# Window attention with a routed feed-forward: score products visit the column halves in turn

## The chip, the cores and the metric

The kernel runs on one core of one Trainium2 chip. The metric is device time in microseconds (us) of one execution. TensorE (PE) does matrix products; it loads a stationary operand (PEld) and then streams a moving operand against it. VectorE is DVE, ScalarE is ACT, GpSimd is POOL, and SyncE (SP) starts most of the DMAs.

## The reference

The input x has 2 images of 128 channels and 256 x 256 pixels, in f32. One layer is computed:

```
x = x + conv(layer_norm_over_channels(x))
t = x as tokens of 128 channels
t = t + ffn(layer_norm(t))
```

`conv` is attention in windows with four heads of 32 channels. Queries come from windows of 8 x 8 pixels, keys and values from overlapping windows of 12 x 12, and a relative position term and a fixed mask are added to the scores:

```
attn = einsum('bnd,bmd->bnm', q * SCALE, k)
attn = attn + rel_pos_emb(q) + FIXED_MASK      # 0 or -inf
attn = softmax(attn);  out = einsum('bnm,bmd->bnd', attn, v);  W_out on top
```

The mask is -inf wherever the row or the column distance of query and key has one of the two parities. A pixel therefore attends only to pixels of fixed row and column parity, and the image falls into four independent planes of half the height and half the width. `ffn` is a routing over 8 experts: softmax, the best two, and the sum of these two experts' products, weighted.

## The kernel before

The image is cut into 64 strips of 8 rows (32 per image). Each strip has 4 planes (the parities), so the main loop runs over 256 steps `n`, one plane each. A plane of a strip has 4 rows of 128 columns, 512 pixels, in 16 windows of 8 columns (`NP = 16`, `HP = 8` of them in each half). A window sees 6 rows of 10 columns of keys, 60 keys, held in a slot of 64 (`SLOT`).

The main loop writes the order of the instructions by hand (a manual schedule over PE, DVE, ACT, Pool and SP), and mixes pieces of several steps: the scores of plane `n`, its attention and output projection, the projections of plane `n + 1`, and the norms, routing and expert products of neighbouring strips. Nothing is reordered by a scheduler. From step 6 on, an alignment at the head of each step puts TensorE's instructions at a fixed place in blocks of 256.

On TensorE a step is, in this order: key-mask products of the scores (L474), score products (L491), value projections (L350), the projections for relative terms, keys and queries (L409, L423, L445), four expert products (L714), softmax sums (L512), attention products (L522), norm statistics (L580), three expert products, the output projection (L550), and a last expert product.

The change touches `scores`. Scores lie with the keys on the partitions: the tile `att` has 128 partitions, 64 for the left half of the windows and 64 for the right half, and four PSUM banks, one for each head. The first 256 columns of a bank hold the queries of 8 windows, 32 each.

- L474 adds the relative terms and the mask. There are two turns `w`, and in each turn 8 products, over `half` and then over head `h`. A product has 32 rows of the array (the head's channels), 64 columns (the slot) and a moving operand of 128 columns.
- L491 adds query times key. For each of the 8 window places `t` there are 8 products, over `half` and then over `h`. A product has the head's 32 rows, 64 columns (the window's keys `kk`) and a moving operand of 32 columns (the window's queries `qs`). Each of the eight pairs (`h`, `half`) is a part of its own in the array: 4 groups of 32 rows by 2 halves of 64 columns. There are 64 such products per step. All products are f32, and each f32 product is two instructions for loading and two for multiplying, in the order load, multiply, load, multiply.
- L499, on ACT, takes the exp of all scores and writes `pT`.

`attend` is not changed. Its L512 and L522 use parts of the other shape: 64 rows (the keys of a half) by 32 columns (a head's channels). L522 has 64 products per step, for each `t` over `half` and then over `h`, each with a moving operand of 32 columns.

Of the kernel before, what the change touches and what calls it, by code (L numbers as in the profile page):

```python
# [18 lines left out]
HEADS, DH = 4, 32  # L19
# [26 lines left out]
SLOT = 64  # L46
# [5 lines left out]
def kernel(  # L52
# [21 lines left out]
    HP = NP // 2  # L74
# [111 lines left out]
    for h in range(HEADS):  # L186
        hp = slice(h * DH, (h + 1) * DH)
# [67 lines left out]
    def place(i, k):  # L255

        return (PR * strips[i][1] + k) % KR
# [204 lines left out]
    def scores(n, state):  # L462


        qs, kk, au = state["qs"], state["kk"], state["au"]
        turn = place(n // 4, 0) // 2
        att = ps_att.tile([P, 4, 512], F32, tag="att", name=f"att{n}")
        sc = att[:, :, 0:HQ]
        for w in range(2):
            for half in range(2):  # L470
                rows = slice(half * SLOT, (half + 1) * SLOT)
                for h in range(HEADS):
                    hp = slice(h * DH, (h + 1) * DH)
                    nc.tensor.matmul(  # L474
                        sc[rows, h].rearrange("p (t w z) -> p t w z", w=2, z=16)[:, :, w],
                        lhsT=keys[hp, turn, w],
                        rhs=au[hp, half * NP + w : (half + 1) * NP : 2].rearrange(
                            "p t a s -> p t (a s)"
                        ),
                        start=(w == 0),  # L480
                        stop=False,
                    )
        for t in range(HP):
            if t == HP // 2:
                yield
            for half in range(2):
                rows = slice(half * SLOT, (half + 1) * SLOT)
                m0 = 2 * (half * HP + t)
                for h in range(HEADS):
                    hp = slice(h * DH, (h + 1) * DH)  # L490
                    nc.tensor.matmul(  # L491
                        sc[rows, h, 32 * t : 32 * t + 32],
                        lhsT=kk[hp, half * HP + t, :],
                        rhs=qs[hp, m0 : m0 + 2].rearrange("p m a s -> p (m a s)"),
                        start=False,
                        stop=(t == HP - 1),
                    )
        pT = work.tile([P, HEADS, HQ], F32, tag="pT", name=f"pT{n}", bufs=1)
        nc.scalar.activation(pT, att[:, :, 0:HQ], AF.Exp)  # L499
        state.update(att=att, pT=pT)  # L500
        yield
# [306 lines left out]
    with tc.manual_schedule(engines={ET.PE, ET.DVE, ET.Activation, ET.Pool, ET.SP}):  # L808
        for n in range(n_planes + 7):
            i, pl = divmod(n, 4)  # L810
            score, attn, outp, ahead, norm, rout = none, none, none, none, none, none
            if n < n_planes:
                score = scores(n, states[n])
                attn = attend(n, states[n])
                outp = out_project(n, states[n])
# [146 lines left out]
```

## Time and profile before

| what | value |
|---|---|
| time, median of 3 runs | 4331.74 us (4326.62 to 4331.98) |
| the profiled execution | 4321.7 us, span 4319.9 us |
| mean granted TensorE clock | 0.992 |
| PE busy | 4217.3 us, 98% of the span |
| PE weight loads busy | 2466.8 us, 57% |
| DVE busy | 3852.5 us, 89% |
| ACT busy | 1452.8 us, 34% |
| POOL busy | 1086.0 us, 25% |
| expert products L714, PE | 1915.4 us in 4096 instructions |
| score products L491, PE | 400.6 us in 32768 instructions |
| attention products L522, PE | 345.1 us in 32768 instructions |
| key-mask products L474, PE | 179.8 us in 8192 instructions |

Busy time is the time in which at least one instruction of a kind is under way; the mean duration of one instruction can be far longer than its share of the busy time, since TensorE works on many small products at once. The span runs from the first to the last instruction of the program. "Releaser" is what ended an engine's wait; "issue" stands for time without a wait that the profile shows.

### The profile page before, as it was taken

The numbers are of one execution on the slowest core, as the hardware profiler recorded it, in microseconds if no ns is written. First come the engines' busy times: TensorE is split into PE (matmuls) and PEld (weight loads), VectorE is DVE, ScalarE is ACT, GpSimd is POOL, SyncE is SP. The second block draws the span as 40 slices with busy tenths as digits, with TensorE's granted clock in tenths as the row PEclk, the third lists the DMA queues.
The fourth block names the chain that finished last, engine by engine and source line by source line (L and its number), as shares of the span: only waits on it lengthen the run. The fifth ranks groups of instructions, "written<-read, shape, count | busy, mean of one in ns | idle before, by whom it ended". The sixth has DMA issues, their size and how long they took to land. (4 is left out here: it accounts for less than half of the span.)

```text
span 4319.9 us, 224653 instructions
## 1 busy us (share of the span) xinstructions
PE 4217.3 (98%) x94273; PEld 2466.8 (57%) x94273; DVE 3852.5 (89%) x11850; ACT 1452.8 (34%) x3774; POOL 1086.0 (25%) x1126
## 2 busy tenths in 40 slices
PE   7899999999999999999999999999999999999987
PEld 4455555555555555555555555555555555555553
DVE  4799999999999999999999999999999999999977
ACT  3333333333333333333333333333333333333321
POOL 1222222222222222222222222222222222222211
PEclk9999999999999999999999999999999999999999
DMA  3678777787777777778787777777778787877765
GB/s 109 209 236 247 240 247 242 241 246 242 245 242 244 247 240 248 243 239 247 241 248 240 246 243 243 245 242 246 241 243 244 240 250 238 247 247 241 243 193 191
DMA packets 824580, 1022.19 MB, mean 237 GB/s; under 512 B 137634, under 2 KB 409634, under 8 KB 823594
## 3 DMA queue, kind: packets, MB, share of 16 engines
q1 hardware_dynamic: 822864, 1007.52, 75.4%
q8 instruction: 769, 12.60, 1.3%
q14 instruction: 217, 1.78, 0.1%
q10 hardware_dynamic: 730, 0.29, 0.0%
HBM read 863.78 MB, written 143.75 MB: 233 GB/s over the span
## 5 line engine op out<-in xcount | busy, mean ns | idle before, releaser
L714 PE MATMUL acc<-xe,ew 128*128 128x512 f32 x4096 | 1915.4, 600 | 18.6 <-DVE gb L688 16.5
L714 PEld LDWEIGHTS acc<-xe,ew 128*128 128x128 f32 x4096 | 758.1, 190 | 936.6 <-issue 886.5
L705 DVE TENSOR_TENSOR xe<-xs,gb 128x512 f32<-128x512 f32 x1536 | 950.6, 686 | 11.1 <-DMA gb<-gd 1.1
L709 POOL COPY last<-xe 128x1 f32<-128x1 f32 x256 | 47.1, 184 | 3113.7 <-DVE gb L688 3107.2
L705 POOL TENSOR_TENSOR xe<-xs,gb 128x512 f32<-128x512 f32 x512 | 650.6, 1272 | 1.5 <-PE att L522 0.7
L491 PE MATMUL att<-qs,kcol 32*64 32x32 f32 x32768 | 400.6, 226 | 11.1 <-issue 10.8
L434 ACT COPY kcol<-pk 128x560 f32<-128x560 f32 (+2 forms) x344 | 318.8, 927 | 275.3 <-PE pk L423 272.5
L491 PEld LDWEIGHTS att<-qs,kcol 32*64 32x64 f32 x32768 | 396.7, 131 | 13.9 <-issue 13.6
L276 POOL TENSOR_TENSOR xn<-xt,rb 128x512 f32<-128x512 f32 x249 | 373.7, 1501 | 91.1 <-DMA rb<-gd 74.6
L522 PEld LDWEIGHTS att<-pT,vwin 64*32 64x32 f32 x32768 | 348.6, 105 | 40.8 <-issue 3.2
L522 PE MATMUL att<-pT,vwin 64*32 64x32 f32 x32768 | 345.1, 200 | 2.4 <-issue 2.2
L499 ACT ACTIVATE pT<-att 128x1024 f32<-128x1024 f32 x256 | 261.9, 1023 | 180.3 <-PE att L491 180.1
L350 PE MATMUL pv<-wt,xn 128*128 128x128 f32 x2048 | 301.1, 291 | 0.9 <-issue 0.9
L574 ACT ACTIVATE sq<-xt 128x512 f32<-128x512 f32 x505 | 291.8, 629 | 0.0
L397 DVE STREAM_TRANSPOSE au<-auT 128x512 f32<-128x512 f32 x256 | 272.1, 1063 | 9.0
L550 PE MATMUL po<-o,wt 128*128 128x512 f32 x512 | 264.9, 599 | 9.5 <-DVE o L542 5.9
L409 PE MATMUL pu<-xn,wrel 128*128 128x512 f32 x512 | 266.2, 602 | 1.2 <-issue 1.2
L445 PE MATMUL pq<-xn,wt 128*128 128x512 f32 x512 | 261.9, 592 | 0.9 <-issue 0.8
L423 PE MATMUL pk<-xn,wt 128*128 128x512 f32 (+2 forms) x528 | 261.4, 578 | 0.0
L350 PEld LDWEIGHTS pv<-wt,xn 128*128 128x128 f32 x2048 | 251.7, 193 | 11.8 <-issue 1.3
L474 PEld LDWEIGHTS att<-au,keys 32*64 32x64 f32 x8192 | 118.9, 132 | 234.0 <-PE po L550 181.1
L413 DVE STREAM_TRANSPOSE uT<-pu 128x512 f32<-128x512 f32 x256 | 177.1, 692 | 65.5 <-PE pu L409 63.6
(2696 smaller groups left out, 4946.0 us busy)
## 6 DMA issues: line engine op xcount, KB each, us to landing
gb<-gd SPq DMA_DIRECT2D x2048, 256.0 KB, 5.5
vwin<-vrows SPq DMA_DIRECT2D x512, 240.0 KB, 5.1
xt<-in_x_dram SPq DMA_DIRECT2D x256, 256.0 KB, 6.5
sb<-gd SPq DMA_DIRECT2D x256, 256.0 KB, 4.1
out_dram<-xt SPq DMA_DIRECT2D x256, 256.0 KB, 6.0
rb<-gd SPq DMA_DIRECT2D x249, 256.0 KB, 3.4
vrows<-vr SPq DMA_DIRECT2D x168, 256.0 KB, 3.8
vrows<-vr SPq DMA_DIRECT2D x160, 128.0 KB, 3.3
```

What stands on the lines that cost most here:

```text
L276: eng.tensor_tensor(xn[i % 2][:, :, :, k, 1 : PC + 1], ln1_src(i, k).rearrange("p (y j x) -> p y x j", y=2, x=2), rb.rearrange("p (y j x) ...
L350: nc.tensor.matmul(pv[:, j * P : (j + 1) * P], lhsT=xp[:, k, 1 : PC + 1], rhs=wv, start=True, stop=True,)
L397: nc.vector.transpose(au.rearrange("p m a s -> p a s m"), auT[n % 2])
L409: nc.tensor.matmul(pu, lhsT=wrel, rhs=inner, start=True, stop=True)
L434: nc.scalar.copy(places[:, 1 : NP - 1], windows(new[:, :, KC - 3 :], 0, NP - 2))
L445: nc.tensor.matmul(pq, lhsT=wq, rhs=inner, start=True, stop=True)
L491: nc.tensor.matmul(sc[rows, h, 32 * t : 32 * t + 32], lhsT=kk[hp, half * HP + t, :], rhs=qs[hp, m0 : m0 + 2].rearrange("p m a s -> p (m a ...
L522: nc.tensor.matmul(av[hp, half, 32 * t : 32 * t + 32], lhsT=vv[rows, t, hp], rhs=pT[rows, h, 32 * t : 32 * t + 32], start=True, stop=True,)
L550: nc.tensor.matmul(po, lhsT=wo, rhs=state["o"].rearrange("p f z -> p (f z)"), start=True, stop=True)
L574: nc.scalar.activation(sq, src, AF.Square)
L705: eng.tensor_tensor(self.xe[e], self.xs, self.gb.pop(e), ALU.mult)
L714: nc.tensor.matmul(self.acc, lhsT=ew[:, e, :], rhs=self.xe.pop(e), start=(e == 0), stop=not self.xe)
```

## The change

The two inner loops of L491's products change places. For one `t`, the eight products ran through the four heads in the left half of the columns and then through the four heads in the right half. Now each head's two halves follow each other. Operands, targets and the number of products are the same, and so are the key-mask products ahead and the exp behind.

```
         for t in range(HP):
             if t == HP // 2:
                 yield
-            for half in range(2):
-                rows = slice(half * SLOT, (half + 1) * SLOT)
-                m0 = 2 * (half * HP + t)
-                for h in range(HEADS):
-                    hp = slice(h * DH, (h + 1) * DH)
+            for h in range(HEADS):
+                hp = slice(h * DH, (h + 1) * DH)
+                for half in range(2):
+                    rows = slice(half * SLOT, (half + 1) * SLOT)
+                    m0 = 2 * (half * HP + t)
                     nc.tensor.matmul(
                         sc[rows, h, 32 * t : 32 * t + 32],
                         lhsT=kk[hp, half * HP + t, :],
```

Written as (head, half), the order of eight products was 00 10 20 30 01 11 21 31 and is now 00 01 10 11 20 21 30 31.

## The prediction

> **What bounds the kernel now.** I read the page first (busy shares, slices), then the busy times by stretch, then the costliest groups, then the timeline of one step, and last the number of weight loads in flight inside the changed stage.
>
> ```profile
> PE 4217.3 (98%) x94273; PEld 2466.8 (57%) x94273; DVE 3852.5 (89%) x11850; ACT 1452.8 (34%) x3774; POOL 1086.0 (25%) x1126
> PE   7899999999999999999999999999999999999987
> PEclk9999999999999999999999999999999999999999
> ```
>
> ```profile
> 500.00:1000.00 500.00, 498.29 (x11231) 291.29 (x11230) 456.57 (x1402) 172.25 (x451) 131.13 (x131) 1.00 0.78 242
> 2000.00:2500.00 500.00, 496.49 (x11226) 291.79 (x11225) 454.96 (x1406) 173.08 (x454) 129.15 (x134) 1.00 0.79 244
> ```
>
> The columns of the second fence are stretch, length, then busy time of PE, PEld, DVE, ACT, POOL, then granted clock and DMA share. The first fence says that TensorE is busy in nearly all of the span, at an undisturbed clock. In the second it is busy 498 of 500 us, at clock 1.00. DVE comes next with 457 of 500. One of the 256 planes takes about 16.3 us (timeline below: score stages begin at 2000.44 and 2016.79), so DVE has about 1.4 us of slack per plane. TensorE's time is the kernel's time: what the score stage gains or loses reaches the end, up to a gain of about 1.4 us per plane.
>
> ```profile
> L491 PE MATMUL att<-qs,kcol 32*64 32x32 f32 x32768 | 400.6, 226 | 11.1 <-issue 10.8
> L491 PEld LDWEIGHTS att<-qs,kcol 32*64 32x64 f32 x32768 | 396.7, 131 | 13.9 <-issue 13.6
> L522 PEld LDWEIGHTS att<-pT,vwin 64*32 64x32 f32 x32768 | 348.6, 105 | 40.8 <-issue 3.2
> L522 PE MATMUL att<-pT,vwin 64*32 64x32 f32 x32768 | 345.1, 200 | 2.4 <-issue 2.2
> ```
>
> L491 is the changed line. Its 16384 products are 32768 pairs of load and matmul: each f32 product is two passes on the same part of the array. 400.6 us over 256 planes is 1.56 us per plane, 9% of the span. A pass lasts 226 ns in the record, yet 128 of them fit in 1.56 us, so many run at once, in eight parts of 32 rows by 64 columns.
>
> **The change, part by part.** It removes nothing and adds nothing. The number of instructions on each engine is the same, and the 64 score products of a plane are the same; DMAs, queues and waits are untouched, and the exp (L499) still waits for the last product. What moves is the order inside one run of 64 products. Before, four neighbours use four row groups of one column half, then four of the other. After, two neighbours use the same 32 rows and differ in the column half. In both orders a part of the array is used again after exactly eight products. So the cost depends on one question: does a product care whether its neighbour shares its rows or its columns?
>
> *Can two parts in the same rows load and run together?* The key-mask products L474 just ahead have the same shape, 32 rows by 64 columns.
>
> ```profile
> 2000.44 0.45 PEld L474 LDWEIGHTS att<-au,keys 32*64 32x64 f32 x32 [0.76 <-PE po L550]
> 2000.44 0.69 PE L474 MATMUL att<-au,keys 32*64 32x128 f32 x32
> ...
> 2000.82 1.52 PEld L491 LDWEIGHTS att<-qs,kcol 32*64 32x64 f32 x128
> 2000.93 1.53 PE L491 MATMUL att<-qs,kcol 32*64 32x32 f32 x128
> ```
>
> ```profile
> 197.11:197.11 0.00, 0.00 (x8) 0.00 (x8) 1.00 0.00 0
> ```
>
> The last fence counts L474's matmuls and loads in flight at one instant (PE, then PEld): eight and eight, before any later load has begun. Eight parts are the whole array, so each row group holds two loads and two matmuls. The single records say what that costs: the eight loads start 6.7 ns apart and last 128 ns each, against 131 for L491's mean; the groups of eight matmuls follow each other every 109 ns, while the full-array passes of the same 128 columns in L350 follow each other every 112 ns. Sharing rows cost nothing there. The second witness is L522, where four neighbours in a row share 64 rows and differ only in the columns: its passes come every 8.3 ns, as fast as any in L491. So I price the pairing at 0 ns. What hides it is that both loads of a row group run side by side; if that cover were gone, the second product of a pair would wait until the first has loaded (55 ns from first to second pass's load in one part, less the 16.7 ns that separate neighbours: 38 ns), 32 pairs times 38 ns is 1.2 us per plane, 313 us in all.
>
> [...]
>
> *What the stage loses today.* Loads of L491 in flight at single instants, and of L522 likewise (the count is in brackets):
>
> ```profile
> 197.96:197.96 0.00, 0.00 (x16) 1.00 0.00 0
> ...
> 198.11:198.11 0.00, 0.00 (x10) 1.00 0.00 0
> ...
> 198.26:198.26 0.00, 0.00 (x15) 1.00 0.00 0
> ...
> 198.46:198.46 0.00, 0.00 (x10) 1.00 5.25 2048
> ...
> 198.61:198.61 0.00, 0.00 (x15) 1.00 0.00 0
> ```
>
> ```profile
> 2010.40:2010.40 0.00, 0.00 (x13) 1.00 0.00 0
> ...
> 2010.80:2010.80 0.00, 0.00 (x13) 1.00 0.00 0
> ```
>
> L522 is flat; L491 dips. From the single records of that plane, first-pass loads come every 16.7 ns except at five places: 79 ns ahead of product 1, 101 ahead of product 9, and 63, 62 and 63 ahead of products 26, 43 and 60. The last three come 17 products apart, so 17 products take 16 x 16.7 + 63 = 330 ns, or 155 ns per eight. Each loses 46 ns, 138 ns per plane, 35 us in all. I do not know what causes them. Two readings differ on what the change does. (a) They follow from the 64-column loads: the second pass's load starts 55 ns after the first's in L491 and 29 ns in L522, so more work stands open between neighbours; the new order keeps that. (b) They follow from four neighbours sharing one column half; the new order ends that. I take (a), because of how long one product holds its part. In L491 the second load starts after 55 ns, takes about as long again, and then a pass streams for about 27 ns (a quarter of L474's 109): 137 ns. In L522 it is 29 + 29 + 27 = 85 ns. The part is wanted again after 8 x 16.7 = 133 ns, so L491 is over that line in either order and L522 far below it.
>
> *Edges.* Product 1 becomes row group 0 of the second half, which the last L474 pass leaves about 27 ns later than the part it replaces; but product 1's load comes 79 ns after product 0's already, so this hides; uncovered, it would be 27 ns x 256 planes = 7 us. At the other end the full-array L350 waits for all eight parts in both orders.
>
> **Sum.** 0 for the pairing, 0 for the dips, 0 for the edges. The profiled execution took 4321.7 us (span 4319.9 and 1.8 around it); it lies 10.0 us below the median of the three runs, 4331.74, which themselves spread from 4326.62 to 4331.98. Adding the sum to the median: 4331 us. About 0.2% (8.7 us, or 34 ns per plane) is what a measurement of this kernel can tell from no change.
>
> **The rivals.** *The dips go (faster).* If reading (b) holds, the three dips vanish: 35 us, 4296 us. For it: L522 has neighbours that share rows, as the new order has, and no dips. Against it: L522's loads are also half as wide. DVE's slack of 1.4 us per plane does not stop a gain of 0.14. The gap ahead of product 9 I leave: at the same place the plane that starts at 1852 us stands still for 0.8 us with no semaphore named, which looks like instruction supply and not order.
>
> *Neighbours in the same rows push each other (slower).* The place is the moving data: a 32-column pass streams for about 27 ns and the neighbour's begins 16.7 ns later, so 10 ns overlap in the same rows, which in the old order meet only the product four places on. If the rows then serve one stream at a time, every round of eight products slips 10 ns: 8 rounds, 80 ns per plane, 20 us (4352). If the slip also makes the queue dip once per round instead of every 17 products, four more dips of 46 ns, 47 us: 4379 us. It decides from a slip of about 4 ns per round on (34 ns per plane). Against it: L474's eight matmuls of 128 columns overlap fully at no cost. The harder case, loads in the same rows one after the other, is the 313 us above; I give it little.
>
> *The change does nothing at all* is the forecast itself: the order is then a relabelling of the eight parts.
>
> **How the numbers follow.** No measurable change gets 0.43 (4323 to 4340), dips gone 0.27 (4296), neighbours pushing each other 0.30, of which 0.08 for prices above 47 us. Witnesses of the very shape speak for the first, but the 17-product dips show a limit in the queue that I cannot name, and an order could touch it either way. The low end is 4296 less the 5 us spread of the runs, 4290; the high end is the 47 us price, 4380. Left out are that 0.08 and about as much for a gain of all five gaps (285 ns per plane, 73 us). Cases of both signs hold more than half, so the likeliest one's own range stands beside it: 4323 to 4340.
>
> **What would show it.** Right: L491's busy time within 8 us of 400.6, its loads in flight still swinging between 16 and 10, gaps of 63 ns still 17 products apart, all other groups unchanged. Faster: L491 near 365 us and a flat count. Slower: L491 at 420 to 450 us, more dips, or loads longer than 131 ns. The forecast is wrong in its core if the pace between dips is no longer 16.7 ns, for then neighbours in one row group do care.

## The result and the profile after

No change that can be measured. The changed kernel took 4329.98 us (median of 4 runs, 4322.56 to 4331.87), the kernel before 4331.86 us in the same comparison (4 runs, 4326.62 to 4332.45); the ratio is 0.9995, with a 95% interval of 0.9978 to 1.0012. The forecast was 4331.0 us, with no measurable change as the likeliest case. That the two lie 1 us apart is luck, since the runs of each kernel spread over 6 to 9 us.

The profiled execution after took 4328.19 us (span 4326.4), against 4321.7 us (4319.9) before. Three views answer those of the prediction: busy shares, one stretch, and the groups of the score and attention products.

```profile
PE 4219.7 (98%) x94273; PEld 2468.7 (57%) x94273; DVE 3856.7 (89%) x11850; ACT 1452.7 (34%) x3774; POOL 1086.3 (25%) x1126
```

```profile
500.00:1000.00 500.00, 497.66 (x11333) 291.80 (x11319) 456.08 (x1409) 171.02 (x449) 131.15 (x131) 1.00 0.80 243
```

```profile
L491 PE MATMUL att<-qs,kcol 32*64 32x32 f32 x32768 | 402.6, 226 | 14.1 <-issue 13.7
...
L491 PEld LDWEIGHTS att<-qs,kcol 32*64 32x64 f32 x32768 | 398.5, 131 | 17.5 <-issue 16.8
...
L522 PE MATMUL att<-pT,vwin 64*32 64x32 f32 x32768 | 345.6, 200 | 2.4 <-issue 1.8
```

The instruction counts are the same, TensorE is as full as it was (98% of the span) at the same clock (0.992), and one pass of L491 still lasts 226 ns and one load 131 ns. L491 is busy 402.6 us instead of 400.6, and its idle time grew by 3 us (14.1 instead of 11.1). Both lie mostly in stalls ahead of product 9, as the single records tell (the start of every load in the trace): in the planes more than 40 ns above the median, the places ahead of product 9 hold 15.0 us of delay before and 20.9 us after. From the start of the first to the start of the last load of the stage the *median* plane takes 1394 ns in both kernels, the *mean* plane 1471.3 ns before and 1491.5 ns after. A second profile of the changed kernel (E9 below) has a median of 1394 and a mean of 1473.4. So these 5 us are a difference between executions and not between orders: 20.2 ns more in the mean plane, times 256, are 5.2 of the 6.5 us by which the two profiled executions differ.

The loads of L491 in flight at single instants of the plane that starts at 194.05 us, taken as in the prediction:

```profile
194.57:194.57 0.00, 0.00 (x16) 1.00 0.00 0
...
194.72:194.72 0.00, 0.00 (x10) 1.00 0.00 0
...
194.87:194.88 0.00, 0.00 (x15) 1.00 5.25 2048
...
195.07:195.07 0.00, 0.00 (x9) 1.00 0.00 0
...
195.22:195.22 0.00, 0.00 (x15) 1.00 0.00 0
```

The count still swings between 16 and about 10. In the single records the first-pass loads still come every 16.7 ns except ahead of product 1 (79 ns), product 9 (101 or 102 ns) and products 26, 43 and 60 (62 to 64 ns). Those are the numbers of before, at the same products.

### The profile page after: what moved, and what is told of

The parts are those of the page before. It is cut to its first block, busy times and chain, and to the rows that moved or that the text cites. A ratio compares the mean times of both kernels' runs of the same rounds, so it can differ in the third digit from the quotient of the medians.

```text
span 4326.4 us, 224653 instructions
## 1 busy us (share of the span) xinstructions
PE 4219.7 (98%) x94273; PEld 2468.7 (57%) x94273; DVE 3856.7 (89%) x11850; ACT 1452.7 (34%) x3774; POOL 1086.3 (25%) x1126
## 5 line engine op out<-in xcount | busy, mean ns | idle before, releaser
L491 PE MATMUL att<-qs,kcol 32*64 32x32 f32 x32768 | 402.6, 226 | 14.1 <-issue 13.7
L491 PEld LDWEIGHTS att<-qs,kcol 32*64 32x64 f32 x32768 | 398.5, 131 | 17.5 <-issue 16.8
L522 PEld LDWEIGHTS att<-pT,vwin 64*32 64x32 f32 x32768 | 348.7, 105 | 41.2 <-issue 3.7
L522 PE MATMUL att<-pT,vwin 64*32 64x32 f32 x32768 | 345.6, 200 | 2.4 <-issue 1.8
L350 PE MATMUL pv<-wt,xn 128*128 128x128 f32 x2048 | 301.0, 290 | 1.0 <-issue 1.0
L409 PE MATMUL pu<-xn,wrel 128*128 128x512 f32 x512 | 266.1, 601 | 0.3 <-issue 0.3
L423 PE MATMUL pk<-xn,wt 128*128 128x512 f32 (+2 forms) x528 | 261.7, 579 | 0.0
L350 PEld LDWEIGHTS pv<-wt,xn 128*128 128x128 f32 x2048 | 251.5, 193 | 11.9 <-issue 1.4
L474 PEld LDWEIGHTS att<-au,keys 32*64 32x64 f32 x8192 | 119.4, 133 | 234.0 <-PE po L550 181.2
```

Of the source, the lines that this page charges most:

```text
L350: nc.tensor.matmul(pv[:, j * P : (j + 1) * P], lhsT=xp[:, k, 1 : PC + 1], rhs=wv, start=True, stop=True,)
L409: nc.tensor.matmul(pu, lhsT=wrel, rhs=inner, start=True, stop=True)
L491: nc.tensor.matmul(sc[rows, h, 32 * t : 32 * t + 32], lhsT=kk[hp, half * HP + t, :], rhs=qs[hp, m0 : m0 + 2].rearrange("p m a s -> p (m a ...
L522: nc.tensor.matmul(av[hp, half, 32 * t : 32 * t + 32], lhsT=vv[rows, t, hp], rhs=pT[rows, h, 32 * t : 32 * t + 32], start=True, stop=True,)
```

## The experiments

Theory R (relabelling): a product does not care which part its neighbour uses; what counts is how soon the same part is wanted again. Rival N (neighbours): parts in the same rows, or in the same column half, hinder each other. A null result of one edit cannot separate "neither matters" from "two effects cancel", so the neighbourhood is varied in both directions and made extreme. Later two readings of the dips at every seventeenth product are set against each other. Each short edit shows the order of products for one `t` as (head, half), unless it says otherwise.

**E1, neighbours never share rows and seldom a column half.** The order goes diagonally, so that a neighbour always differs in the row group and, in six of the eight steps of a round, in the column half as well.

```
-00 10 20 30 01 11 21 31
+00 11 20 31 01 10 21 30
```

> The eight score products of one window place run so that neighbours differ in both the rows and the column half (as head, half: 00 11 20 31 01 10 21 30). Theory R (relabelling: the eight parts of the array do not care who their neighbour is; only how soon a part comes again counts, and here it is eight products again): no change, ratio to before 0.998 to 1.002, L491 busy 398 to 405 us, gaps of 63 ns ahead of products 26, 43 and 60. Rival N (neighbourhood: sharing a column half costs something and sharing rows costs about the same, so that the change only swapped one for the other): this order has neither, so L491 falls towards 365 us and the kernel by up to 35 us (ratio 0.992).

Measured: 4321.35 us (10 runs) against 4320.45, ratio 0.9999 [0.9989, 1.0008] (here and below in brackets the 95% interval). The group of the score products:

```profile
L491 PE MATMUL att<-qs,kcol 32*64 32x32 f32 x32768 | 400.8, 226 | 10.4 <-issue 9.7
```

The median plane takes 1390.5 ns from first to last load, 3.5 ns less than before, or 0.9 us in all. The order that should have helped if shared rows or shared columns cost anything brings nothing.

**E2, the change in all four tiled loops.** L474, L512 and L522 get the head outside and the half inside too.

```
+            for h in range(HEADS):
+                hp = slice(h * DH, (h + 1) * DH)
+                for half in range(2):
...
```

> The change made in all four attention lines: score products as in the change, and also the key-mask products (L474), the softmax sums and the attention products with head outside and half inside. Theory R: no change anywhere, ratio 0.998 to 1.002, L474 within 4 us of 180, L522 within 4 us of 345. Rival N: L522 today has four neighbours in the same rows and no dips; with halves alternating, neighbours share a column group instead, and it should gain dips or lose pace: 64 products with three dips of 20 to 46 ns, +15 to +35 us.

Measured: 4326.23 us against 4320.45, ratio 1.0013 [1.0003, 1.0024]; 5.6 us, just outside equality and below the 0.2% that I called measurable.

```profile
L522 PE MATMUL att<-pT,vwin 64*32 64x32 f32 x32768 | 345.3, 200 | 2.4 <-issue 1.8
...
L474 PE MATMUL att<-au,keys 32*64 32x128 f32 x8192 | 180.7, 283 | 35.5 <-issue 34.6
```

In the single records L474, L512 and L522 take as long from their first to their last load as before (319, 75 and 1334 ns in the median plane), within 1 ns. The score stage's mean plane is 1488 ns against 1471, and L491's idle time is 13.8 us against 11.1, while one load still lasts 131 ns: this points to long stalls in some planes again, and not to the pace. Whether the small slowdown is a real effect (a stall met more often) or the luck of the executions, these runs do not settle.

**E3 and E4, a part wanted again after four products.** The same 64 products, reordered over `t`: four parts take turns for two `t`, then the other four, so that a part comes back after 4 products and then after 12. In E3 the four parts lie in two row groups and both column halves, in E4 in four row groups of one column half. R says that the two agree; N says that the one whose rows are shared, or the one whose columns are shared, is worse.

```
+        for t2 in range(0, HP, 2):
...
+            for h2 in range(0, HEADS, 2):            # E3
+                for t in (t2, t2 + 1):
+                    for h in (h2, h2 + 1):
+                        for half in range(2):
...
+            for half in range(2):                     # E4
+                for t in (t2, t2 + 1):
+                    for h in range(HEADS):
```

> For two window places together: heads 0 and 1 in both halves for the first place, then for the second, then heads 2 and 3 likewise. A part comes again after 4 products (and then after 12). Theory R: a part is held 137 ns and wanted after 4 x 16.7 = 67 ns, so queues form; if all is paced by four parts, 137/4 = 34 ns per product, 64 x (34 - 19.4) = 0.95 us per plane, +240 us; if the queue lets the next four parts go ahead, much less, from 0 on. In any case the same as the kernel with four parts in one column half (the other run with distance 4), within 0.3%. Rival N: the two differ by over 0.5%, since here four neighbours sit in two row groups and there in four.

> For two window places together: the four heads in the left half for the first place, then for the second, then the right half likewise. A part comes again after 4 products (and then after 12), as in the other run with distance 4, but the four parts lie in one column half and in all four row groups. Theory R: the same time as that run within 0.3%, and somewhere between 0 and +240 us above before. Rival N: differs from it by over 0.5%.

Measured: E3 4346.22 us, ratio 1.0053 [1.0035, 1.0071]; E4 4346.25 us, ratio 1.0055 [1.0040, 1.0071]. The two groups (the line moved with the loops):

```profile
L493 PE MATMUL att<-qs,kcol 32*64 32x32 f32 x32768 | 429.2, 223 | 11.3 <-issue 10.8
```

```profile
L492 PE MATMUL att<-qs,kcol 32*64 32x32 f32 x32768 | 427.7, 223 | 5.8 <-issue 5.7
```

Both median planes take 1493 ns, 99 ns more than before. 99 ns times 256 planes is 25.3 us; the medians differ by 25.8 us. So the distance at which a part comes back costs something, what lies beside it costs nothing, and most of what this stage loses reaches the end of the kernel. That the two sums agree to half a us is luck: the intervals reach from 15 to 31 us and from 17 to 31 us.

**E7 and E8, a part wanted again after two products.** In E7 the two parts are the halves of one head, and eight neighbours in a row share one row group; in E8 they are two heads in one half, and eight neighbours share one column half and two row groups. In both a part comes back three times after 2 products and then after 26.

```
+        for t4 in range(0, HP, 4):
...
+            for h in range(HEADS):                    # E7
+                for t in range(t4, t4 + 4):
+                    for half in range(2):
...
+            for half in range(2):                     # E8
+                for h2 in range(0, HEADS, 2):
+                    for t in range(t4, t4 + 4):
+                        for h in (h2, h2 + 1):
```

> For four window places together one head after the other, each in both halves: a part comes again after 2 products, four times, and the eight products in a row lie in one row group. Theory R: the queue seen so far reaches about 17 products, so two heads' four parts work side by side: 4 products in 110 to 137 ns each part, 28 to 34 ns per product instead of 19.4, +0.55 to +0.95 us per plane, +140 to +240 us, ratio 1.03 to 1.055, and the same within 0.3% as the kernel with two parts of one column half. Rival N: rows shared by all eight neighbours cost more than the column half shared, over 0.5% apart.

> For four window places together two heads in one half, then the other two heads, then the other half: a part comes again after 2 products, four times, and the eight products in a row lie in one column half and two row groups. Theory R: +140 to +240 us, and the same within 0.3% as the run with one row group. Rival N: over 0.5% apart.

Measured: E7 4606.79 us, ratio 1.066 [1.0638, 1.0683]; E8 4583.67 us, ratio 1.0615 [1.0589, 1.0641]. The groups of the score products and of the first projection behind them, E7 first:

```profile
L492 PE MATMUL att<-qs,kcol 32*64 32x32 f32 x32768 | 670.7, 223 | 6.0 <-issue 5.5
...
L409 PE MATMUL pu<-xn,wrel 128*128 128x512 f32 x512 | 286.2, 643 | 0.0
```

```profile
L493 PE MATMUL att<-qs,kcol 32*64 32x32 f32 x32768 | 662.8, 221 | 4.8 <-issue 4.2
...
L409 PE MATMUL pu<-xn,wrel 128*128 128x512 f32 x512 | 272.5, 615 | 0.0
```

The median plane takes 2351 ns in E7 and 2348 ns in E8. That is 957 and 954 ns more than before, 245 and 244 us over 256 planes, of the 285 and 261 us that the medians rose. With its long planes the stage's busy time grew by 270 and 262 us (670.7 and 662.8 against 400.6). R had expected 140 to 240 us, from a queue that reaches about 17 products; that reach was R's estimate from the distance of the dips, and no run shows it. Both whole times lie above R's range, and the stage alone at its upper end. At the stage itself the two agree within 3 ns, even though E7 puts eight neighbours into one row group. Yet the kernels differ by 23.1 us, just over 0.5%: that is more than the 0.3% that R allowed, and by the whole times alone it is the sign of N. Between the two profiled executions TensorE's busy time differs by 40 us (4532.5 and 4492.5); the score products hold only 8 of them. The larger part comes from full-array passes, some of which took far longer than the others: L409, L350 and L423 together are busy 32.5 us longer in E7 than in E8. L409's mean is 643 ns in E7, 615 in E8 and 602 before, and 54, 23 and 10 of its passes were slow. The ten of before took over 700 ns instead of the median 595; seven of them took 1061 ns, and the granted clock of the trace was 0.50 during each of these seven (4136.97 to 4138.03 us is one). The granted clock over the span is 0.977 in E7's profile and 0.986 in E8's. One such place in E7, by timeline and then by stretches (start and end, length, PE busy, PEld, DVE, ACT, POOL, then the granted clock):

```profile
1053.11 0.62 PE L492 MATMUL att<-qs,kcol 32*64 32x32 f32 x17
1054.08 2.25 PE L492 MATMUL att<-qs,kcol 32*64 32x32 f32 x111 [0.35 <-issue]
...
1057.43 1.91 PE L409 MATMUL pu<-xn,wrel 128*128 128x512 f32 x2
```

```profile
1053.00:1056.30 3.30, 2.95 (x153) 2.79 (x137) 2.94 (x13) 0.31 (x2) 0.00 (x0) 1.00 0.96 354
1056.50:1060.50 4.00, 4.00 (x12) 2.28 (x12) 1.12 (x4) 1.57 (x3) 0.00 (x0) 0.57 0.31 101
1061.00:1065.00 4.00, 4.00 (x10) 1.52 (x8) 3.97 (x8) 3.24 (x8) 0.00 (x0) 1.00 0.55 161
```

After a stall ahead of product 9 and a stage with only two parts at work, the granted clock is 0.57 on average over 4.00 us, and L409's pass takes 1061 ns instead of 595. What lowers the clock is not shown: TensorE was busy in 2.95 of the 3.30 us ahead and paused for 0.35 us. Why E7 has more slow passes of L409 than E8 (54 against 23), with equal paces, stays open, and with it whether the parts that work side by side have a hand in it.

**E5 and E6, narrower loads in the order of before.** Each window has 60 keys in a slot of 64. E5 loads 60 columns, which drops only the padding. E6 loads 48 and leaves out query times key for the last two of the ten key columns. Here reading (a) of the prediction (a part is held longer than the 133 ns after which it is wanted) expects the dips to go once the load is short enough. Rival C says that they follow from a count in TensorE's queue, every 17 products or 68 instructions, and stay.

```
-                        sc[rows, h, 32 * t : 32 * t + 32],
-                        lhsT=kk[hp, half * HP + t, :],
+                        sc[half * SLOT : half * SLOT + 60, h, 32 * t : 32 * t + 32],   # E6: 48
+                        lhsT=kk[hp, half * HP + t, 0:60],                              # E6: 0:48
```

> The order of before, but each score product loads and writes 60 columns and not 64 (the four padding columns of a slot hold zero weights, so the result is the same). Reading (a) of the dips (a part is held longer than the 133 ns after which it is wanted): the second load starts after about 52 ns and the part is held 2 x 52 + 27 = 131 ns, under the line; the three dips go, L491 falls by 35 us to 365 and the kernel to a ratio of 0.992. Rival C (the dips come every 17 products whatever a load takes, a count in the queue): they stay and shrink by the 3 ns that the second load comes sooner, 3 x 3 ns per plane, ratio 0.999 to 1.000.

> The order of before, 48 columns of each slot (the keys of the last two of ten columns of a window get no product with the query: that part of the scores is left out). Reading (a): held 2 x 41 + 27 = 109 ns, far under the line, no dips, ratio 0.991 to 0.992, the count of loads in flight flat as in L522. Rival C: dips of 63 - 14 = 49 ns ahead of products 26, 43 and 60 stay, 33 ns lost in each, ratio 0.997.

Measured: E5 4316.43 us against 4322.28, ratio 0.9987 [0.9977, 0.9997]; E6 4308.16 us, ratio 0.9961 [0.9949, 0.9973]. E5, then E6:

```profile
L491 PE MATMUL att<-qs,kcol 32*60 32x32 f32 x32768 | 395.5, 224 | 16.1 <-issue 15.7
```

```profile
L491 PE MATMUL att<-qs,kcol 32*48 32x32 f32 x32768 | 372.7, 213 | 11.4 <-issue 11.0
```

The median plane takes 1369 ns and 1299 ns. The dips stay at products 26, 43 and 60 in both kernels, and only shrink: 63 ns with 64 columns, 56 with 60, 36 with 48, about 1.7 ns for each column. There is no line at which they end. C is right that they stay, but mis-sized the shrinkage: it expected 49 ns at 48 columns. Product 9 lies 17 products ahead of product 26, so it stands in the same series of places; but its gap stays 101 to 102 ns at 60 and at 48 columns, so width does not set that one. If the same slope held down to L522's 32 columns, the gap would be about 9 ns, less than the 16.7 ns of the ordinary pace; that is an argument for why L522 is flat, and no run shows it. What holds the loads back at every seventeenth product is not settled.

E6 also shows where a gain stops. Its stage became 95 ns shorter in the median plane and 94 ns in the mean one, or 24 us, but the median time fell by 14.1 us and the span of the profiled execution by 17.4 us. The missing part is idle time ahead of the key-mask products, 7 us more than before; before and then in E6:

```profile
L474 PE MATMUL att<-au,keys 32*64 32x128 f32 x8192 | 179.8, 282 | 35.4 <-issue 34.4
```

```profile
L474 PE MATMUL att<-au,keys 32*64 32x128 f32 x8192 | 180.4, 283 | 42.3 <-issue 40.2
```

In the single records, from one score stage to the next, three of the four steps of a strip are 108 ns shorter than before in the median. The first step of a strip is 126 ns longer (16.47 us instead of 16.35): it ends in this wait, and before it already did so a little. What TensorE waits for there is not named in the profile.

**E9 and E10, the change again, and the change with 60 columns.**

```
+            for h in range(HEADS):                    # E9, E10: the order of the change
+                hp = slice(h * DH, (h + 1) * DH)
+                for half in range(2):
...
+                        lhsT=kk[hp, half * HP + t, 0:NK],        # E10 only
```

> The changed kernel itself once more, in more rounds, to narrow the interval. Theory R: ratio 0.999 to 1.001, L491 busy 398 to 405 us. Any real effect of the order of over 0.1% would show as an interval that leaves 1.000 out.

> The order of the change together with 60 columns instead of 64. Theory R: the order adds nothing, so it is the run with 60 columns again: ratio 0.998 to 0.9995, L491 busy near 395 us, gaps of about 56 ns ahead of products 26, 43 and 60. Rival N: the two edits together differ from the 60 columns alone by over 0.2%.

Measured, against 4325.13 us before: E9 4323.57 us (11 runs), ratio 0.9995 [0.9985, 1.0006]; E10 4317.58 us (10 runs), ratio 0.998 [0.997, 0.999]. The group of E10:

```profile
L491 PE MATMUL att<-qs,kcol 32*60 32x32 f32 x32768 | 397.1, 223 | 12.9 <-issue 12.1
```

E9 narrows the interval of the change: at most 0.15% faster and 0.06% slower. E10's median plane is 1371 ns, as E5's 1369. The gain comes from the width and is the same in both orders, as far as these intervals tell. E5 and E10 beat the kernel before by 0.1% and 0.2%, with intervals that leave out no change; E10's median is also 0.1% below that of the changed kernel, measured beside it as E9. E6 is faster still, but leaves out part of the scores.

## Why the prediction was right, point by point

- **TensorE's time is the kernel's time, up to a gain of 1.4 us per plane.** The first half is shown: E3 and E4 added 25.3 us in the stage and 25.8 us to the end. The bound on gains was wrong. It came from DVE's average slack, but in E6 a gain of 0.095 us per plane was already lost in one step of four; of 24 us in the stage 17 us reached the end of the profiled execution. In E5, with 6.4 us in the stage (25 ns x 256) and 5.9 us at the end, the loss is too small to be seen: the interval reaches from 1 to 10 us. So the 35 us of the dips would probably not all have come through either. The forecast does not suffer, since it had no gain to pass on.
- **Pairing at 0 ns.** Shown for the stage. The pace between dips stayed 16.7 ns, E1 (no rows shared with a neighbour) gained nothing, E2 paired L474 and L522 too with their pace unchanged, and with eight neighbours in one row group E7 ran the stage within 3 ns of E8. What the pairing of parts does to the clock, the 0.5% between E7 and E8, is open; the changed kernel's clock was 0.992 as before.
- **Neighbours pushing each other, 20 to 47 us.** It fell. The 10 ns of overlapping streams in the same rows cost nothing: the changed order has the pace and the dips of before, and E3 and E4 share rows differently and have the same 1493 ns. The rival's upper price was also added up short: the slip and the extra dips together are 20 + 47 = 67 us, not 47.
- **The dips go, 35 us.** It fell, and the reason is now better known. Reading (b), four neighbours in one column half, is out: the change ended that, and the dips stayed at the same products with the same 63 ns.
- **Reading (a).** The conclusion held that a new order keeps the dips, but the step behind it did not. The comparison of 137 ns against 133 ns made the width a threshold. E6 brings a part's hold well under 133 ns (two loads of 41 ns, 48/64 of 55, and 27 ns of streaming: 110 ns by the same sum), and the dips are still there at 36 ns; they shrink steadily with the width instead. So the 0 for the dips came out right from a wrong reason; as far as this step goes, that was luck.
- **Return after eight products.** The prediction named this as what both orders keep. E3, E4, E7 and E8 show that it is the variable that matters: 1394 ns with a return after eight, 1493 after four and then twelve, about 2350 after two, three times, and then twenty-six.
- **Edges at 0.** Shown: product 1 still comes 79 ns after product 0, and L474's group is unchanged within 1 us (180.8, before 179.8). At the other end the first load of L350 starts 41 ns after the last load of L491 ends, in the median plane of both orders.
- **L491 within 8 us of 400.6.** It was 402.6, and 402.3 in E9. The gap ahead of product 9, left out as instruction supply and not order, did stay at the same product in both orders. Its cause was argued, not shown: its place is 17 products ahead of the first of the three dips, so it may have to do with them.

## What to carry to other kernels

With small products in tiles of the array, ask first after how many products the same tile comes back: here eight and the order of neighbours within them did not matter, while two cost 245 us in the stage alone. An order that kept this distance was a relabelling here, and columns of padding in a load were worth more than any reordering of neighbours (4 of 64 columns: 0.1% to 0.2%). Before counting on a gain, look at the longest step and not at the average slack of the next engine: one step in four gave back what it had won. When an edit seems to do nothing, make it extreme in both directions before believing it, and compare median stages by single records as well as whole times, since stalls in some planes move a group's busy and idle time together by 4.6 us from one execution to the next (L491 in the two profiles of the changed kernel: 416.7 and 412.1 us).

## What was not expected of the hardware

- A gap in the loads ahead of every seventeenth f32 product (68 instructions) of the score stage, from product 9 on, in the order of before and in that of the change. At products 26, 43 and 60 it is 63 ns at 64 columns and loses about 1.7 ns per column taken away; at product 9 it is about 101 ns at every width tried.
- Long stalls, most of them ahead of product 9 (in 31 planes before and 41 after): 40 of the 256 planes before and 51 after lie more than 40 ns above the median plane, by 19 and 24 us in all and by up to 1.7 us in one plane. They are what differs in this stage between the two profiles of the changed kernel: 1394 ns in the median plane of both, 1491.5 and 1473.4 ns in the mean one.
- More slow passes behind a sparser stage: 54 passes of L409 in E7 and 23 in E8 were slow, against 10 before (means 643, 615 and 602 ns; granted clock over the span 0.977, 0.986 and 0.992), and two kernels with the same pace in the changed stage differ by 0.5%.
